# The first residual loads and three sums of leaves behind the first router, and the last block product added straight to the output

## The chip, the cores and the metric

The kernel runs on one core of a Trainium2 chip. The core has TensorE (matrix products, written PE in the profile, with its weight loads as PEld), VectorE (DVE), ScalarE (ACT), GpSimd (POOL) and SyncE (SP). SP, ACT and POOL also start DMA transfers, which move data between the memory of the chip and the core. All arithmetic here is in 32-bit floats.

The metric is the time of one execution on the device in microseconds, as the median of several runs. The profile comes from one further execution, and its times are counted from the start of its span.

## The reference

4096 tokens of width 1024 come in groups of 64; each group picks one of 16 matrices of 64 x 64, which mixes its 64 rows. On the mixed rows a router picks 16 of 64 experts per token, and two matrix products with gates between them are added to the input:

```python
W = weights[condition]                          # (64, 64, 64)
z = jnp.einsum('bct,bcd->bdt', x, W)            # mixed rows, 4096 x 1024
scores = z @ Wr.T                               # 64 experts
top_vals, top_idx = jax.lax.top_k(scores, 16)
gates = jax.nn.softmax(top_vals, axis=-1)       # scattered to G (4096 x 64)
h = jnp.einsum('nd,krd->nkr', z, A)             # 64 experts x rank 16 = 1024
out = jnp.einsum('nkr,kdr->nd', h * G[:, :, None], B)
return x + 2.0 * out
```

So the kernel computes two products of 1024 x 1024 for each token (by A, then by B) with the mixing, the router and the gates between them, and a sum with the residual x.

## The kernel before, in words

The tokens are worked on in 8 groups of 512. For each group there are two stages, `h` (x by A) and `o` (gated h by B). A stage is a product of 2 x 2 blocks, made from 7 block products p1 to p7 by the Strassen-Winograd scheme: sums of blocks go in, sums of products come out. The blocks of h are 256 tokens by 512 columns. From the second group on each of the 7 products is cut once more into 2 x 2 blocks and made from 7 "leaves" (so 49 small products for a stage); in the first group the products are whole (`whole_parent`, L529), while the sums of the leaves of A and B for all later groups are made and stored to memory beside them.

**The order of the work.** It is written out by hand. All products stand in one list `parents` (h0, o0, h1, h2, o1, h3, o2, and so on, o7 last), and `run` (L581) goes through them one after another. Each product has hooks: `mid`, `late` and `end` are lists of small jobs that `run` calls at three places of the product. `at(n, when, f, ...)` (L849) puts a job into a list. Each engine does its instructions in the order in which the program issues them, so a job's place in these lists is its place in the queue of its engine.

**In the first group,** with `h` and `o` the numbers of the first products of the two stages:

- `gather` (L153) starts the loads of the mixing matrices on POOL; `scores_t`, `turn`, `scores` (L172 to L230) make the router's scores.
- `route_top` (L232, at h+3) takes the 8 largest scores on VectorE, `exps` (L247) the exponentials on ScalarE, and `rest` (L257, at h+4) the next 8 with the sums and their reciprocals on VectorE. `scaled` (L285) multiplies the gates on ScalarE. `gates` (L297, at h+5) turns them with four transposes on TensorE (`gp`, L301), and `gated` (L308) mixes a quarter of z with 64 small products (`zp`, L321) and multiplies it by the gates on VectorE (`hb`, L334).
- `b_steps` (L890) is the list of the sums of leaves of B, 4 to each of the 7 products. Each is one subtraction on VectorE of 128 x 512 into a tile of the pool `bsum` (5 tiles), followed by a store to memory by POOL (`step`, L409, store at L414). `steps_of(lst, n)` takes the next n from the list. The table at L959 gives their places.
- `load_res` (L733) loads quarters of the residual x, 512 KB each, in the first group with POOL's queue, in later groups with SP's. They are added to on VectorE and stored as the output.

**A product of the second level** (`parent`, L474) has three accumulators x, y, w in the banks of TensorE. Its order in `run`: leaf p1 to x, ScalarE copies x to `r1`; p2 to y, VectorE makes the (0,0) quarter of the product as y + r1 (`part`, L603); then leaf p3 of the product before (`third`, L606), p6 on top of x and its copy `a`; leaf p4 of the product before (`fourth`, L610), whose quarter is w + a; p7 to w, p5 on top of x and its copy `b`, and the quarter (1,1) as w + b. The quarter (0,1) is x after p3. Then `done` of the product before adds it to its parts of the output, in `o_parents` (L776).

**The end.** The last product is p3 of the stage o of group 7. Its place in the output is the (0,1) quarter, an `o` tile of 2 x 128 tokens by 512. `finish` (L652) takes the quarters (0,0) and (1,1) from the product's tile, adds these and the copies a and b to the output, then makes leaf p3 in a bank of its own (`last_z`) and p4 on top of w, adds both, and stores the two halves with SP and ACT (L661). `late` (L786) adds product p5 to that quarter once p2, p5 and p4 are there.

Of the kernel before, what the change touches and what calls it, by code (L numbers as in the profile page):

```python
# [15 lines left out]
P = 128  # L16
BANK = 512
# [3 lines left out]
TPG = 4  # L21
CH = 4
HN = TPG * P // 2
HALF = BANK // 2
# [5 lines left out]
def kernel(  # L30
# [26 lines left out]
    nc = tc.nc  # L57
# [6 lines left out]
    NG = NT // TPG  # L64
# [21 lines left out]
    def add(o, a, b):  # L86
        nc.vector.tensor_tensor(o, a, b, ALU.add)  # L87
# [355 lines left out]
    parents, to_fetch, ring, stay, fetched = [], [], [], {}, [0]  # L443
# [137 lines left out]
    def run(par, before, after, hooks):  # L581


        two = par and par["level"] == 2
        tail = before and before["level"] == 2

        def bank(n):
            par["bank"][n] = acc.tile(
                [P, par["width"]],
                F32,  # L590
                tag="acc",
                name=f"{par['kind']}_{par['g']}_{par['j']}_{n}",
            )
            return par["bank"][n]

        def copied(n):
            lt = pools["lt"].tile(
                [P, HALF + KC], F32, tag=n, name=f"l_{n}", bufs=2 if n == "a" else 1
            )
            par["val"][n] = lt[:, : par["width"]]  # L600
            nc.scalar.copy(par["val"][n], par["bank"]["x"])  # L601

        def part(pr, i, j, n, v):  # L603
            add(pr["q"][i][j], pr["bank"][n], pr["val"][v])

        def third():  # L606
            before["mm"](before["bank"]["x"], "p3", False)
            nc.scalar.copy(before["q"][0][1], before["bank"]["x"])  # L608

        def fourth():  # L610
            before["mm"](before["bank"]["w"], "p4", False)
            part(before, 1, 0, "w", "a")

        if par:
            par["begin"]()
        if two:
            par["mm"](bank("x"), "p1", True)
            copied("r1")
            par["mm"](bank("y"), "p2", True)
            part(par, 0, 0, "y", "r1")  # L620
        elif par and hooks["both"]:
            par["both"]()
        elif par:
            par["half"](0)
        if before and not tail:
            before["done"](before["m"], before["v"])
        if tail:
            third()
        if two:
            par["mm"](par["bank"]["x"], "p6", False)  # L630
            copied("a")
        if tail:
            fourth()
        for f in hooks["mid"]:
            f()
        if after and after["level"] == 2:
            after["prepare"]()
        for f in hooks["late"]:
            f()
        if two:  # L640
            par["mm"](bank("w"), "p7", True)
            par["mm"](par["bank"]["x"], "p5", False)
            copied("b")
            part(par, 1, 1, "w", "b")
        elif par and not hooks["both"]:
            par["half"](1)
        if tail:
            before["done"](before["m"], before["v"])
        for f in hooks["end"]:
            f()  # L650

    def finish(par, st):  # L652

        o, q = st["os"][0, 1], par["q"]
        for s, k, v in ((0, 0, q[0][0]), (1, 1, q[1][1]), (0, 1, par["val"]["b"]), (1, 0, par["val"]["a"])):
            add(o[:, s, ts(k, HALF)], o[:, s, ts(k, HALF)], v)
        z = acc.tile([P, HALF], F32, tag="acc", name="last_z")
        for s, k, p, b, queue in ((0, 1, "p3", z, nc.sync), (1, 0, "p4", par["bank"]["w"], nc.scalar)):
            par["mm"](b, p, p == "p3")
            add(o[:, s, ts(k, HALF)], b, o[:, s, ts(k, HALF)])  # L660
            queue.dma_start(out[ts(st["g"] * TPG + s, P), ts(1, BANK)], o[:, s, :])  # L661

    def add_piled(o, piles, n):
        for s in range(2):
# [78 lines left out]
    def store(st, i, j):  # L743
        (nc.sync if st["g"] else nc.gpsimd).dma_start(
            out[ds((st["g"] * TPG + 2 * i) * P, 2 * P), ts(j, BANK)].rearrange(
                "(s p) t -> p s t", p=P
            ),
            st["os"][i, j],
        )
# [26 lines left out]
    def o_parents(st):  # L776

        m_ = {}

        def into(i, j, t, last=False):  # L780
            o = st["os"][i, j]
            add(o, o, t)
            if last:
                store(st, i, j)

        def late():  # L786
            if {"p2", "p5", "p4"} <= m_.keys():
                into(0, 1, m_["p5"])

        def done(j):  # L790
            def f(m, v):
                m_[j] = m
                if j == "p1":
                    into(0, 0, m)
                elif j == "p2":
                    into(0, 0, m, True)
                    late()
                elif j == "p6":
                    add(m_["p1"], m_["p1"], m)
                    into(1, 0, m_["p1"], {"p7", "p4"} <= m_.keys())  # L800
                elif j == "p4":
                    into(1, 0, m, {"p7", "p6"} <= m_.keys())
                    late()
                elif j == "p7":
                    into(1, 1, m)
                    into(1, 0, m, {"p4", "p6"} <= m_.keys())
                elif j == "p5":
                    assert {"p6", "p7"} <= m_.keys()
                    add(m, m, m_["p1"])
                    into(1, 1, m, True)  # L810
                    late()
                else:
                    into(0, 1, m, True)

            return f

        return [parent("o", st, j, lambda: st["h_ops"], done(j)) for j in ORDER["o"]]
# [14 lines left out]
    sts = [{"g": g} for g in range(NG)]  # L832
    for k, g in (
# [4 lines left out]
        st = sts[g]  # L838
# [10 lines left out]
    def at(n, when, f, *args):  # L849
        hooks[n][when].append(lambda: f(*args))  # L850
# [34 lines left out]
    def steps_of(lst, n):  # L885
# [4 lines left out]
    b_steps = [  # L890
        f for j in ("p1", "p2", "p3", "p7", "p5", "p6", "p4") for f in leaf_steps("o", j, br[j])
    ]
# [25 lines left out]
    st = sts[0]  # L918
    h, o = st["h"], st["o"]
# [38 lines left out]
    at(o + 3, "end", b_sums, 4)  # L958
    for k, lst, n in (  # L959
        (h + 2, b_steps, 4),  # L960
        (h + 3, b_steps, 5),
        (h + 4, b_steps, 3),
        (h + 5, a_steps, 4),
        (h + 6, a_steps, 5),
        (o, a_steps, 2),
        (o + 1, b_steps, 7),
        (o + 2, a_steps, 7),
        (o + 3, b_steps, 1),
        (o + 3, a_steps, 2),
        (o + 4, b_steps, 6),  # L970
        (o + 5, b_steps, 2),
    ):
        at(k, "end", steps_of, lst, n)
# [8 lines left out]
    h = sts[1]["h"]  # L982
# [5 lines left out]
    for st in sts[1:]:  # L988
        n, g = st["h"] + 7, st["g"]
# [33 lines left out]
    for st in sts:  # L1023
        g, h, o = st["g"], st["h"], st["o"]
        if not g:
            at(h + 2, "mid", load_res, st, (0, 0), (1, 1), (1, 0))
            at(o + 5, "mid", load_res, st, (0, 1))
        else:
            at(h - 1, "mid", x_operands, st)
            at(h + 1, "mid" if g < 3 else "late", sums, st, "x_sums", "s3")  # L1030
            at(h + 1, "end", sums, st, "x_sums", "s2")
            at(h + 2, "end", sums, st, "x_sums", "s1")
            at(h + 3, "end", sums, st, "x_sums", "s4")
            at(o - 2, "end", h_operands, st)
            at(o - 1, "end", sums, st, "h_sums", "s3")
            at(o + 0, "end", sums, st, "h_sums", "s2")
            at(o + 1, "end", sums, st, "h_sums", "s1")
            at(o + 3, "late", sums, st, "h_sums", "s4")
            for k, q in zip((-2, -1, 1, 2), QUARTERS):
                at(o + k if g + 1 == NG else o - 4, "mid", load_res, st, q)  # L1040
            if g + 1 < NG:
                at(h + 3, "mid", gather, g + 1)
                at(h + 3, "end", load_x, g + 1, 0, 0)
                at(h + 4, "end", load_x, g + 1, 1, 0)
                at(h + 5, "mid", load_x, g + 1, 1, 1)
                at(h + 6, "mid", load_x, g + 1, 0, 1)
    for n, par in enumerate(parents):
        if n == sts[1]["h"]:
            steady()
        after = parents[n + 1] if n + 1 < len(parents) else None  # L1050
        run(par, parents[n - 1] if n else None, after, hooks[n])
    finish(parents[-1], sts[-1])


_OUT = (64, 64, 1024)
# [41 lines left out]
```

## Time and profile before

| | us |
|---|---|
| median of 3 runs | 784.57 |
| the three runs | 784.48, 784.57, 785.79 |
| the profiled execution, its own time | 786.72 |
| its span, first to last instruction | 784.8 |
| TensorE busy | 772.8 |
| VectorE busy | 623.7 |
| ScalarE busy | 184.7 |
| DMA, mean rate | 266 GB/s |

Mean granted clock of TensorE over the span: 0.995 of full speed.

How to read it: part 1 of the page gives the busy time of each engine as a share of the span; part 2 cuts the span into 40 slices of 19.6 us and gives the busy share of each in tenths. Rows of the timeline give start, length, engine, line, operation, output <- inputs, shapes and count; a bracket holds the time that the engine stood idle before the row and what ended that. A line such as L87 or L90 belongs to a helper (`add`, `sub`), so rows are told apart by their tiles: `os_p_p` is a sum of leaves of B, `hs_p_p` one of A, `o_p_p` and `h_p_p` their places in memory, `lo_p_p` and `lh_p_p` the leaves loaded again, `l_r`, `l_a`, `l_b` the copies r1, a and b, `m_o_p` a product of the stage o, `o` a quarter of the output. Rows of the waits give the waiting engine and line, what ended the wait, the sum in us, how many and the longest. q1 is the DMA queue of SP, q0 that of POOL, q10 that of ACT.

### The profile page before, as it was taken

To read this page: it belongs to the slowest core of one execution; us is meant where nothing else is said; L and a number is where in the kernel's file an instruction comes from. 1 tells how busy PE (TensorE), PEld (TensorE's weight loads), DVE (VectorE), ACT (ScalarE), POOL (GpSimd) and SP (SyncE) were. 2 spreads that over 40 slices of the span, in tenths; PEclk is the share of its full clock that TensorE was granted. 3 is DMA by queue.
4 is the path that set the end of the run, shared out by engine and by line. 5 is a ranking of instruction groups with operands and counts; after the bars stand their busy time and mean duration, and the time that the engine had idled before them with its cause. 6 is when DMAs were issued, how large, how long until landed. Compare 5 with 4: busy or idle time off the path is not lost.

```text
span 784.8 us, 14669 instructions
## 1 busy us (share of the span) xinstructions
PE 772.8 (98%) x5348; PEld 612.4 (78%) x5348; DVE 623.7 (79%) x1310; ACT 184.7 (24%) x490; POOL 74.3 (9%) x103
## 2 busy tenths in 40 slices
PE   9989999999999999999999999999999999999996
PEld 5444448888888888887888888888888888888885
DVE  4788975678788868897788976888768887788986
ACT  1120002223122222322222222222222231222221
POOL 4334352000200020000200010000200000000000
PEclk9999999999999999999999999999999999999998
DMA  9968579656788858886788958799488893688995
GB/s 332 403 256 296 202 235 316 192 166 208 237 265 286 298 191 295 280 299 236 240 283 284 311 199 283 261 291 334 130 315 269 283 352 119 221 261 255 353 377 215
DMA packets 107607, 208.50 MB, mean 266 GB/s; under 512 B 11072, under 2 KB 27200, under 8 KB 106640
## 3 DMA queue, kind: packets, MB, share of 16 engines
q1 hardware_dynamic: 100496, 186.83, 70.7%
q0 software_dynamic: 6608, 19.95, 7.3%
q8 instruction: 43, 0.70, 0.4%
q10 hardware_dynamic: 432, 0.79, 0.3%
q14 instruction: 28, 0.23, 0.1%
HBM read 174.41 MB, written 33.11 MB: 264 GB/s over the span
## 4 chain that ended last, share of the span: by engine, by line
PE 90%; DVE 3%; issue 3%; POOL 2%; DMA 2%; ACT 0%; POOLq 0%; DVEq 0%
PE h_p_x L508 23%; PE o_p_x L508 20%; PE h_p_w L508 12%; PE o_p_w L508 10%; PE h_p_y L508 6%; PE o_p_y L508 5%; PE zp L321 4%; PE o_x L545 4%; PE o_w L545 2%; POOL w_st L157 1%; PE gp L301 1%; DMA cond_b<-in_cond_dram 1%; DVE o L87 1%; PE sw L221 1%; PE o_y L545 1%
## 5 line engine op out<-in xcount | busy, mean ns | idle before, releaser
L508 PE MATMUL o_p_x<-lo_p_p,l_t 128*128 128x256 f32 x584 | 142.8, 379 | 0.0
L508 PEld LDWEIGHTS o_p_x<-lo_p_p,l_t 128*128 128x128 f32 x584 | 111.0, 190 | 15.4
L87 DVE TENSOR_TENSOR o<-o,m_o_p 128x1024 f32<-128x1024 f32 (+1 forms) x67 | 78.8, 1194 | 0.9 <-DMA o<-in_x_dram 0.4
L157 POOL DMA_INDIRECT w_st<-in_cw_dram,idx x32 | 34.9, 1090 | 429.4 <-PE zp L321 413.4
L87 DVE TENSOR_TENSOR m_h_p<-h_p_w,l_a 128x272 f32<-128x272 f32 x49 | 21.5, 439 | 62.6 <-PE h_p_w L508 62.6
L87 DVE TENSOR_TENSOR m_h_p<-m_h_p,m_h_p 128x1088 f32<-128x1088 f32 x49 | 62.3, 1282 | 0.2
L508 PE MATMUL h_p_x<-a,l_t 128*128 128x272 f32 x224 | 60.5, 392 | 0.0
L508 PE MATMUL h_p_w<-lh_p_p,l_t 128*128 128x272 f32 x196 | 53.8, 397 | 0.0
L508 PE MATMUL h_p_x<-lh_p_p,l_t 128*128 128x272 f32 x196 | 52.9, 392 | 0.0
L508 PE MATMUL o_p_w<-lo_p_p,l_t 128*128 128x256 f32 x196 | 51.1, 383 | 0.0
L508 PEld LDWEIGHTS h_p_x<-a,l_t 128*128 128x128 f32 x224 | 42.6, 190 | 8.6
L334 DVE TENSOR_TENSOR hb<-zp,gg 128x512 f32<-128x512 f32 x64 | 39.9, 683 | 9.8 <-PE zp L321 9.8
L601 ACT COPY l_b<-h_p_x 128x272 f32<-128x272 f32 x49 | 18.9, 386 | 121.8 <-PE h_p_x L508 119.5
L508 PE MATMUL h_p_x<-at,l_t 128*128 128x272 f32 x168 | 45.4, 392 | 0.0
L508 PEld LDWEIGHTS h_p_x<-lh_p_p,l_t 128*128 128x128 f32 x196 | 37.2, 190 | 7.5
L601 ACT COPY l_b<-o_p_x 128x256 f32<-128x256 f32 x49 | 18.2, 372 | 103.8 <-PE o_p_x L508 103.8
L508 PEld LDWEIGHTS h_p_w<-lh_p_p,l_t 128*128 128x128 f32 x196 | 36.5, 191 | 7.0
L508 PEld LDWEIGHTS o_p_w<-lo_p_p,l_t 128*128 128x128 f32 x196 | 36.6, 190 | 5.2
L321 PEld LDWEIGHTS zp<-w_st,m_h_p 64*64 64x64 f32 x2048 | 32.5, 137 | 7.9 <-issue 7.7
L87 DVE TENSOR_TENSOR m_o_p<-o_p_w,l_a 128x256 f32<-128x256 f32 x48 | 20.3, 422 | 22.8 <-PE o_p_w L508 22.8
L508 PEld LDWEIGHTS h_p_x<-at,l_t 128*128 128x128 f32 x168 | 31.9, 190 | 6.6
L608 ACT COPY m_h_p<-h_p_x 128x272 f32<-128x272 f32 x49 | 18.9, 386 | 70.7 <-PE h_p_x L508 70.7
(172 smaller groups left out, 1387.9 us busy)
## 6 DMA issues: line engine op xcount, KB each, us to landing
lo_p_p<-o_p_p SPq DMA_DIRECT2D x280, 256.0 KB, 3.9
lh_p_p<-h_p_p SPq DMA_DIRECT2D x147, 272.0 KB, 5.3
lo_p_p<-in_b_t_dram SPq DMA_DIRECT2D x63, 256.0 KB, 4.0
x<-in_x_t_dram SPq DMA_DIRECT2D x31, 512.0 KB, 5.8
o<-in_x_dram SPq DMA_DIRECT2D x28, 512.0 KB, 7.3
out_dram<-o SPq DMA_DIRECT2D x27, 512.0 KB, 5.0
o_p_p<-os_p_p POOLq DMA_DIRECT2D x28, 256.0 KB, 4.0
b<-in_b_t_dram SPq DMA_DIRECT2D x4, 1024.0 KB, 19.6
```

The costliest lines, as they stand in the source:

```text
L87: nc.vector.tensor_tensor(o, a, b, ALU.add)
L157: nc.gpsimd.indirect_dma_start(out=w_st[:, i, :], out_offset=None, in_=cw, in_offset=bass.IndirectOffsetOnAxis(ap=idx[:, n : n + 1], axis=0),)
L221: nc.tensor.matmul(sw[r, i, ts(k, K // 2)].rearrange("p (d k) -> p d k", d=2), lhsT=ws[g][r, i, :], rhs=halves(st["z"][i // 2, k])[r, i % ...
L301: nc.tensor.transpose(gp[:, i, :], st["g2"][i].rearrange("p a k -> p (a k)"), ident)
L321: nc.tensor.matmul(zp[b][e * D : (e + 1) * D, c, s, :], lhsT=halves(z)[r, s, c // 2, ds(c % 2 * P + e * D, D)], rhs=ws[g][r, 2 * i + s, :] ...
L334: nc.vector.tensor_tensor(tokens(hb[j, i])[:, :, :, b, :], zp[b], g_ij[:, :, :, b, :], ALU.mult)
L508: nc.tensor.matmul(bank, lhsT=v[:, c, :], rhs=w[:, c, :width], start=first and c == 0, stop=c == 1, skip_group_check=True,)
L545: nc.tensor.matmul(piles[n, s], lhsT=left()[j][:, c, ts(s, P)], rhs=w, start=c == 0 and PILES[kind][j].isupper(), stop=c == CH - 1, skip_g ...
L601: nc.scalar.copy(par["val"][n], par["bank"]["x"])
L608: nc.scalar.copy(before["q"][0][1], before["bank"]["x"])
```

## The change

It has two places.

In the first group, the loads of three quarters of the residual move from the `mid` jobs of product h+2 to those of h+6, and three of the sums of leaves of B from the `end` jobs of h+3 to those of h+4. The number of loads, sums and stores stays as it was.

At the end, `run` treats the last product in another way. Its leaf p2 and its copy r1 are added to the output's (0,0) part by two adds, instead of being summed in the product's tile first. The step behind `after["prepare"]` goes to `finish` at once, after the product before has been added (`before["done"]`). `finish` adds the copy a, makes leaves p7 and p5 itself, adds w to the part (1,1), makes p3 and p4, and then adds b, the bank of p3, b again and w, with each half stored when its last add is done. `late` of the last group doesn't wait for p2 any longer, so p5 is added to the (0,1) quarter one product earlier.

```diff
@@ run
             par["mm"](bank("y"), "p2", True)
-            part(par, 0, 0, "y", "r1")
+            par["copied"] = copied
+            if after is None:
+                o = sts[-1]["os"][0, 1][:, 0, :HALF]
+                add(o, o, par["bank"]["y"])
+                add(o, o, par["val"]["r1"])
+            else:
+                part(par, 0, 0, "y", "r1")
...
+        if after is None:
+            before["done"](before["m"], before["v"])
+            bank("w")
+            return finish(par, before, sts[-1])
         if two:
             par["mm"](bank("w"), "p7", True)
@@ finish
-    def finish(par, st):
-
-        o, q = st["os"][0, 1], par["q"]
-        for s, k, v in ((0, 0, q[0][0]), (1, 1, q[1][1]), (0, 1, par["val"]["b"]), (1, 0, par["val"]["a"])):
+    def finish(par, before, st):
+
+        o, q, val = st["os"][0, 1], par["q"], par["val"]
+
+        def into(s, k, v):
             add(o[:, s, ts(k, HALF)], o[:, s, ts(k, HALF)], v)
+
+        def out_tile(s, queue):
+            queue.dma_start(out[ts(st["g"] * TPG + s, P), ts(1, BANK)], o[:, s, :])
+
+        into(1, 0, val["a"])
+        par["mm"](par["bank"]["w"], "p7", True)
+        par["mm"](par["bank"]["x"], "p5", False)
+        par["copied"]("b")
+        into(1, 1, par["bank"]["w"])
         z = acc.tile([P, HALF], F32, tag="acc", name="last_z")
-        for s, k, p, b, queue in ((0, 1, "p3", z, nc.sync), (1, 0, "p4", par["bank"]["w"], nc.scalar)):
-            par["mm"](b, p, p == "p3")
-            add(o[:, s, ts(k, HALF)], b, o[:, s, ts(k, HALF)])
-            queue.dma_start(out[ts(st["g"] * TPG + s, P), ts(1, BANK)], o[:, s, :])
+        par["mm"](z, "p3", True)
+        par["mm"](par["bank"]["w"], "p4", False)
+        into(0, 1, val["b"])
+        into(0, 1, z)
+        out_tile(0, nc.sync)
+        into(1, 1, val["b"])
+        into(1, 0, par["bank"]["w"])
+        out_tile(1, nc.scalar)
@@ o_parents, late
-            if {"p2", "p5", "p4"} <= m_.keys():
+            if {"p5", "p4"} | ({"p2"} if st["g"] + 1 < NG else set()) <= m_.keys() and "late" not in m_:
+                m_["late"] = True
                 into(0, 1, m_["p5"])
@@ the table of the sums of leaves
         (h + 2, b_steps, 4),
-        (h + 3, b_steps, 5),
-        (h + 4, b_steps, 3),
+        (h + 3, b_steps, 2),
+        (h + 4, b_steps, 6),
@@ the loads of the residual
-            at(h + 2, "mid", load_res, st, (0, 0), (1, 1), (1, 0))
+            at(h + 6, "mid", load_res, st, (0, 0), (1, 1), (1, 0))
             at(o + 5, "mid", load_res, st, (0, 1))
@@ the main loop
         run(par, parents[n - 1] if n else None, after, hooks[n])
-    finish(parents[-1], sts[-1])
```

## The prediction

> **What bounds the kernel now.** I began with the page's first two parts, to see which engine fills the span and where it doesn't.
>
> ```profile
> PE 772.8 (98%) x5348; PEld 612.4 (78%) x5348; DVE 623.7 (79%) x1310; ACT 184.7 (24%) x490; POOL 74.3 (9%) x103
> ...
> PE   9989999999999999999999999999999999999996
> ```
>
> TensorE is busy for 98% of the span, and its only thin slices are the third (39 to 59 us) and the last (765 to 785 us). The change removes no matmul, so it can gain only there. The waits of TensorE in the first 150 us come next; after that, no TensorE wait is longer than 0.4 us.
>
> ```profile
> PE gp L301 <- ACT g L289: 2.6, 1, 2.6
> ```
>
> The timeline of TensorE around this wait, with start, length, and in brackets the idle time before it and its releaser:
>
> ```profile
> 39.26 10.46 PE L545 MATMUL h_x<-at,x 128*128 128x512 f32 x24
> 52.28 1.21 PE L301 MATMUL gp<-ident,g 128*128 128x128 f32 x4 [2.56 <-ACT g L289]
> 53.42 1.99 PE L321 MATMUL zp<-w_st,m_h_p 64*64 64x64 f32 x64
> 55.34 4.39 PE L545 MATMUL h_x<-at,x 128*128 128x512 f32 x8
> 59.57 7.03 PE L545 MATMUL h_w<-a,sum_p 128*128 128x512 f32 x16
> ```
>
> TensorE stands still for 2.56 us until the gates of the first router arrive, and what follows is slow too: the 64 small products take 1.91 us from start to start, against 1.09 us for the same 64 at 69.96 us. The table by stretches has the granted clock in the column after POOL:
>
> ```profile
> 50.00:52.00 2.00, 0.00 (x0) 0.00 (x0) 1.74 (x12) 0.17 (x1) 0.00 (x0) 1.00 0.48 193
> 52.00:54.00 2.00, 1.72 (x24) 1.14 (x28) 2.00 (x2) 2.00 (x6) 0.00 (x0) 0.84 0.01 2
> 54.00:56.00 2.00, 2.00 (x56) 1.71 (x50) 1.97 (x4) 0.11 (x1) 0.94 (x2) 0.50 0.04 12
> ```
>
> The clock falls to half after the wait. Who makes the gates late is read from VectorE's timeline:
>
> ```profile
> 33.19 0.69 DVE L90 TENSOR_TENSOR os_p_p<-b 128x512 f32<-128x512 f32 x1 [1.11 <-DMA b<-in_b_t_dram]
> 33.91 1.42 DVE L90 TENSOR_TENSOR os_p_p<-b,os_p_p 128x512 f32<-128x512 f32 x2
> 40.36 0.69 DVE L90 TENSOR_TENSOR os_p_p<-b 128x512 f32<-128x512 f32 x1 [5.03 <-DMA o_p_p<-os_p_p]
> 40.97 0.60 DVE L243 MAX8 tops<-sc 128x8 f32<-128x64 f32 x4
> ...
> 45.86 0.69 DVE L90 TENSOR_TENSOR os_p_p<-b 128x512 f32<-128x512 f32 x1 [0.31 <-DMA o_p_p<-os_p_p]
> ```
>
> The scores had been ready since 32.8 us. The router waits in VectorE's queue behind a sum of leaves that stands 5.03 us for a buffer, whose store (GpSimd's queue, issued at 34.18 us) has to land. Two shares of the DMA time between 28 and 30 us show why that is slow (packets, MB, share of the 16 engines):
>
> ```profile
> q1 hardware_dynamic: 71, 0.53, 65.8%
> q0 software_dynamic: 72, 0.29, 37.1%
> ```
>
> The engines are full, and q0 is then carrying the three residual loads of 512 KB, issued at 22.67 us, the last of which takes 13.4 us to land; the leaf stores queue behind them. At the other end, VectorE's last rows:
>
> ```profile
> 776.37 3.14 DVE L87 TENSOR_TENSOR o<-o,m_o_p 128x1024 f32<-128x1024 f32 x4
> 779.43 0.42 DVE L87 TENSOR_TENSOR o<-o,l_b 128x256 f32<-128x256 f32 x1
> 779.77 0.42 DVE L87 TENSOR_TENSOR o<-o,l_a 128x256 f32<-128x256 f32 x1
> 780.10 0.42 DVE L87 TENSOR_TENSOR o<-last_z,o 128x256 f32<-128x256 f32 x1
> 780.44 0.41 DVE L87 TENSOR_TENSOR o<-o_p_w,o 128x256 f32<-128x256 f32 x1
> ```
>
> TensorE's last product ends at 777.64 us, but VectorE still adds until 780.85 us; the last store is issued at 780.88 us and lands 2.8 us later. VectorE sets the end.
>
> **Part 1, residual loads moved (`load_res` from h+2 to h+6).** Three loads leave GpSimd's queue ahead of all leaf stores and reappear behind twelve leaf stores and nine raw or h-leaf stores. Of the 1.5 MB, some 0.95 MB moved before 33.1 us (0.23, 0.29 and 0.25 in the stretches of 2 us from 26 to 32, the rest after); at about 0.40 MB per us, block b11 lands some 2.4 us sooner, at about 30.7 us, which is before VectorE is free (32.08 us). So the first three sums start at 32.1 us instead of 33.19: 1.1 us. The first leaf store is then issued at about 33.1 us with nothing ahead of it in q0. Its landing time isn't shown for that state. From below it is 2.8 us (the stores at 54.5 to 56 us, engines idle), from above 6.2 us (the store at 34.18 us with the loads still ahead of it). I take 4.5 us, the store issued at 41.35 us: SP's backlog beside it, no loads ahead. It lands at 37.6 us, so the fourth sum starts there and not at 40.36: 2.8 us earlier (4.5 to 1.1 for the two bounds).
>
> **Part 2, three sums moved behind the router.** 3 x 0.69 us and the 0.31 us wait at 45.86 leave the path before `rest`: from 43.5 to 46.47 us as it stood, 2.3 us. With part 1, `rest` starts 5.1 us earlier, at 41.4; the reciprocals end at 46.7 instead of 51.79 us. ScalarE first finishes a copy at 46.92 us (its row at 46.33, bound to TensorE), then makes the four gates by 48.2 us, and TensorE reaches the transposes at 49.6 us. The wait is gone with 1.4 us to spare. With the 6.2 us landing the first gate is there at 48.9: still no wait.
>
> The gain on TensorE, from 49.56 us (39.26 plus 24 matmuls at 0.429) to the row at 59.57: 10.0 us before. After: 4 transposes some 0.6 (weight loads of 0.138 each), 1.09 for zp, 3.63 for 8 matmuls behind a zp (71.05 to 74.68): 5.3 to 5.6. That is 4.4 to 4.7 us: 2.56 of wait, 0.5 of transposes paced by ScalarE, and about 1.5 of half clock (0.82 in zp, 0.60 in h_x).
>
> **A rule that weighs against the last term.** The row: half clock for 3.4 us, from about 53.4 to 56.8 (0.68 in the stretch of 1 us from 53, 0.50 in the two behind it, 0.62 in that from 56). The Trainium skill, "TensorE: Matmul & The Clock Gate", Part 1 (What's actually happening), says that the clock drops to 4/8 after an idle window of about 3.4 us and that this window runs free of the kernel's start. The length agrees with the row. But the gap here is only 2.56 us (3.7 with the sparse transposes), so by the rule another run, with the window lying otherwise, need not drop at all. By the row the drop is worth 1.5 us in each run; by the rule anything from 0 to 1.5 in the timed ones, and the three timed runs, 784.48, 784.57 and 785.79, are apart by about that much. No run here shows the clock of a timed run. I take 0.9 for the median.
>
> **Where the moved work goes.** VectorE has no idle time from 46.5 to 70.36 us, so I followed it on. The six sums now stand together before the adds to `m_h_p` and `hb` (49.0 to 53.3 us); with five buffers the sixth waits for the store of the first: 0 to 1.5 us. hb00 ends at 55.7 to 57.4 us; TensorE needs it at 66.43 - 4.6 = 61.8. VectorE is through with the h leaves at 67.9 (66.2 to 69.6); TensorE's second block product of the next stage (75.77 us) then needs the gated hb and its sum, 2.54 us of VectorE, by 71.1: VectorE has to be free by 68.4. It costs 0 to 1.2 us; I take 0.3. The residual loads, 3 x 0.75 us of GpSimd, now go out at about 64 to 66 us; behind them stand four h leaf stores and three raw leaves, which nobody needs before 77 us. The first residual is added at about 75 us; even with 9.5 us to landing it is there.
>
> **Part 3, the tail.** The add of p5 into the (0,1) quarter moves up into the pause at 772.7 to 773.9 us, where VectorE waited 0.77 us. The (0,0) quarter is no longer first made in `m`: one add of 0.42 and the later add become two, at 773.97 and 774.42. Then in VectorE's order: p4 of the product before 774.76; the 1024-wide add 775.2; `a` 776.34; bank w 776.68 to 777.10. TensorE's last product has to wait for this read (it overwrites the bank), so it starts at 777.16 instead of 776.51: 0.65 us lost, it ends at 778.29. Meanwhile `b` 777.02, z 777.46, `b` again 777.80; the last add waits for TensorE and runs 778.4 to 778.8. The last store is issued at 778.85, against 780.88: 2.0 us. Two small adds more than before (0.34 each) are inside. The stores are the same in number; the 512 KB one goes out 1.15 us earlier, and the 2.8 us to landing stay. Bounds: 1.4 us, if each dependent add costs another 0.1, to 2.3.
>
> **Sum.** Against the profiled execution (span 784.8, time 786.72): 3.1 + 1.5 - 0.3 + 2.0 = 6.3, so 780.4 us. The median of the timed runs is 2.15 us below the profiled one; with the half-clock term at 0.9 the gain is 5.7, and 784.57 - 5.7 = 778.9 us.
>
> **Rivals.**
> - Both parts work: 0.70. 778.9 us, own range 777.3 to 780.4.
> - The early gain is given back, since VectorE arrives late at the next stage or the wait for a buffer turns up again ahead of the router: only the tail is left, 784.57 - 2.0 to 2.8, about 782. For it: the landing of a store is the least known number, and VectorE's slack was 0.8 us at 71.16. Against it: the three sums alone, 2.3 us, nearly cover the 2.56. 0.12.
> - The tail gains nothing, since TensorE's new wait for the read of bank w and the chain of adds into one tile eat it: 784.57 - 3.7 = 780.9. Against it: 3.2 us lie between TensorE's end and VectorE's. 0.06.
> - No change that can be measured: both terms fail. 784.6. 0.05.
> - Slower: the first residual lands so late that VectorE, blocked in order at its add, delays hb10, which TensorE needs at 90.90 - 4.6 = 86.3 us. Each us after about 84.7 costs one us, and the gains of 5.7 are used up at 90.4 us, 27 us after the issue. The longest landing shown for these loads is 13.4 us. From 92 us on it would be past 786.2. 0.07.
>
> **How the numbers follow.** The predicted time is that of the first case. The range starts at 777.2 (all of the clock term, nothing late, and 0.3 of spread) and reaches to 782.3, which takes in the two half-gains; outside remain the last two cases and a rest of the others. 0.2% is 1.6 us, about what a measurement of this kernel can tell from no change. Faster: 0.70 + 0.11 + 0.06 = 0.87; the same: 0.06; slower: 0.07.
>
> **What would show it.** The wait of TensorE for g at L301 below 0.5 us and the clock at 1.00 from 50 to 60 us; the wait of 5.03 us for o_p_p near 2.5 to 3.5; MAX8 at about 38 us; the row h_w behind it at about 55 us; no new TensorE wait before 90 us. In the last 10 us, a wait of TensorE for VectorE of about 1.1 us before the last o_p_w, and 1.2 us from TensorE's end to the last store's issue. I'm wrong if the leaf store still takes over 6 us without the loads ahead of it, if TensorE stands at the second product of the o stage, or if a dependent add into the same tile costs clearly more than 0.42 us.

## The result, and the profile after

The changed kernel takes 780.6 us (median of 6 runs, 779.68 to 781.05) against 785.59 us for the kernel before on the same chip (6 runs, 784.48 to 786.71): a ratio of 0.9936, 95% interval 0.9923 to 0.9948, or 5.0 us less. The profiled execution took 780.21 us, with a span of 778.4 us against 784.8: 6.4 us less.

The first two parts of the page of the changed kernel, lines as in the prediction:

```profile
PE 770.6 (99%) x5348; PEld 610.9 (78%) x5348; DVE 623.8 (80%) x1310; ACT 184.5 (24%) x490; POOL 73.8 (9%) x103
...
PE   9999999999999999999999999999999999999997
```

The third slice is full. The waits of TensorE in the whole span, without one of 1.5 us at its very start that both kernels have, and below the dots the old one (total, number, longest):

```profile
PE o_p_w L508 <- DVE o L87: 0.9, 1, 0.9
PE h_w L545 <- DVE m_h_p L87: 0.7, 1, 0.7
...
PE gp L301 <- ACT g L289: 0.2, 1, 0.2
```

The wait for the gates is 0.2 us instead of 2.6. Two waits are new: one at the row `h_w` in the first group, and one before the last product. The timeline of TensorE shows the first of them in place:

```profile
39.31 10.46 PE L545 MATMUL h_x<-at,x 128*128 128x512 f32 x24
49.61 0.60 PE L301 MATMUL gp<-ident,g 128*128 128x128 f32 x4
50.14 1.16 PE L321 MATMUL zp<-w_st,m_h_p 64*64 64x64 f32 x64
51.23 3.70 PE L545 MATMUL h_x<-at,x 128*128 128x512 f32 x8
55.66 7.13 PE L545 MATMUL h_w<-a,sum_p 128*128 128x512 f32 x16 [0.73 <-DVE m_h_p L87]
```

The transposes follow the 24 products at once, and the 64 small products take 1.09 us from start to start, where they took 1.9. The granted clock, again in the column after POOL in the table by stretches, stays at full speed:

```profile
50.00:52.00 2.00, 2.00 (x68) 1.52 (x68) 2.00 (x4) 0.88 (x2) 0.40 (x1) 1.00 0.03 8
52.00:54.00 2.00, 2.00 (x6) 0.85 (x5) 1.89 (x3) 0.00 (x0) 1.69 (x4) 1.00 0.58 211
54.00:56.00 2.00, 1.27 (x4) 0.40 (x3) 1.68 (x3) 0.58 (x1) 1.30 (x4) 1.00 0.95 350
```

But the row `h_w` starts at 55.66 us, 3.9 us earlier than before (59.57), and not 4.6. What went otherwise is in VectorE's timeline:

```profile
31.99 0.69 DVE L90 TENSOR_TENSOR os_p_p<-b 128x512 f32<-128x512 f32 x1
32.72 1.42 DVE L90 TENSOR_TENSOR os_p_p<-b,os_p_p 128x512 f32<-128x512 f32 x2
39.73 0.69 DVE L90 TENSOR_TENSOR os_p_p<-b 128x512 f32<-128x512 f32 x1 [5.60 <-DMA o_p_p<-os_p_p]
40.34 0.60 DVE L243 MAX8 tops<-sc 128x8 f32<-128x64 f32 x4
...
54.32 0.69 DVE L90 TENSOR_TENSOR os_p_p<-b 128x512 f32<-128x512 f32 x1 [0.36 <-DMA o_p_p<-os_p_p]
54.93 1.28 DVE L87 TENSOR_TENSOR m_h_p<-m_h_p,h_w 128x512 f32<-128x512 f32 x2
```

The wait ahead of the router is still there. It has grown from 5.03 to 5.60 us, so MAX8 starts 0.6 us earlier than before, where I had 2.8. The router is ready in time only because three sums no longer stand between MAX8 and the reciprocals (experiment 2 puts them back). The six sums behind the router then push the adds to `m_h_p` to 54.93 us, and TensorE waits for the bank that these read.

The end of VectorE's and TensorE's work, with the issues of the last two stores:

```profile
771.65 1.23 DVE L87 TENSOR_TENSOR o<-o,m_o_p 128x1024 f32<-128x1024 f32 x1
...
773.46 0.42 DVE L87 TENSOR_TENSOR o<-o,l_b 128x256 f32<-128x256 f32 x1
773.60 1.13 PE L508 MATMUL o_p_w<-lo_p_p,sum_p 128*128 128x256 f32 x4 [0.93 <-DVE o L87]
...
774.77 0.42 DVE L87 TENSOR_TENSOR o<-o,o_p_w 128x256 f32<-128x256 f32 x1
775.22 0.35 ACTq L670 DMA_DIRECT2D out_dram<-o  x1
```

The 1024-wide add is out of the way early. TensorE waits 0.93 us, and one small add is left behind its last product.

**Where the 6.4 us come from.** TensorE is 3.91 us earlier at the row `h_w`, and still 3.80 us earlier at the first row of the second group (114.57 against 118.37). From the start of `last_z` to the issue of the last store it took 5.46 us before (775.42 to 780.88) and takes 3.57 now (771.65 to 775.22): 1.89 less. From that issue to the end of the span it was 3.92 us, now 3.18. The differences make 3.80 + 1.89 + 0.74 = 6.4. The last of them is no gain of the change: in the profiles of the experiments this time is 3.2 to 3.9 us.

### The profile page after: what moved, and what is told of

Same layout as the page of the kernel before. It is cut to its first block, busy times and chain, and to the rows that moved or that the text cites. A ratio compares the mean times of both kernels' runs of the same rounds, so it can differ in the third digit from the quotient of the medians.

```text
span 778.4 us, 14669 instructions
## 1 busy us (share of the span) xinstructions
PE 770.6 (99%) x5348; PEld 610.9 (78%) x5348; DVE 623.8 (80%) x1310; ACT 184.5 (24%) x490; POOL 73.8 (9%) x103
## 4 chain that ended last, share of the span: by engine, by line
PE 95%; DVE 3%; DMA 1%; issue 0%; ACT 0%; ACTq 0%; DVEq 0%
PE h_p_x L508 23%; PE o_p_x L508 20%; PE h_p_w L508 12%; PE o_p_w L508 10%; PE h_p_y L508 6%; PE o_p_y L508 5%; PE zp L321 4%; PE o_x L545 4%; PE h_x L545 3%; PE h_w L545 2%; PE o_w L545 2%; DMA x<-in_x_t_dram 1%; DVE o L87 1%; PE sw L221 1%; PE gp L301 1%; PE h_y L545 1%
## 5 line engine op out<-in xcount | busy, mean ns | idle before, releaser
L87 DVE TENSOR_TENSOR o<-o,m_o_p 128x1024 f32<-128x1024 f32 x65 | 78.0, 1219 | 0.6
```

## The experiments

Every time is compared with the kernel before in the same session. Its median moved between 784.7 and 786.2 us from session to session; the seventh experiment shows what may lie behind it.

**1. Only the loads back.** If the residual's loads hold up the leaf stores, putting them back must make the wait ahead of the router longer.

```diff
-            at(h + 6, "mid", load_res, st, (0, 0), (1, 1), (1, 0))
+            at(h + 2, "mid", load_res, st, (0, 0), (1, 1), (1, 0))
```

> The changed kernel with the three residual loads back at h+2; the sums of leaves and the end stay changed. My prediction (the loads hold up the first leaf store in q0) expects VectorE's fourth sum some 3 to 4 us later than it would be without the loads. The rival, from the profile of the changed kernel (the wait there is 5.60 us, no shorter): the loads don't matter for that wait; the fourth sum starts at about 40.4 us against 39.7, rest about 0.6 us later, and TensorE's wait for m_h_p grows from 0.7 to some 1.3 us. Then the span is 778.7 to 779.3 us and the time at most 1 us above that of the changed kernel.

Measured: 781.24 us (4 runs), ratio 0.9947 (0.9927 to 0.9966), which isn't told apart from the change's 0.9936. VectorE's timeline:

```profile
31.95 0.69 DVE L90 TENSOR_TENSOR os_p_p<-b 128x512 f32<-128x512 f32 x1
...
38.90 0.69 DVE L90 TENSOR_TENSOR os_p_p<-b 128x512 f32<-128x512 f32 x1 [4.80 <-DMA o_p_p<-os_p_p]
...
42.49 0.69 DVE L90 TENSOR_TENSOR os_p_p<-b,os_p_p 128x512 f32<-128x512 f32 x1 [0.45 <-DMA h_p_p<-hs_p_p]
```

With the loads ahead of it the first leaf store lands no later: the fourth sum starts at 38.90 us, even earlier than in the changed kernel. So taking the loads away shortened nothing, and my step for part 1 falls. This doesn't show that the loads hold up nothing where they are present: by the landings in the trace the store lands here at 38.88 us, 1.0 us behind the last of the three loads (37.87), and in the kernel before at 40.34, 1.9 us behind it (38.47), as in a queue that is worked off in order. It shows that without the loads something else holds the store as long. The first sums start at 31.95 us in this run too, so their earlier start isn't the loads' alone either.

**2. Only the sums back.**

```diff
-        (h + 3, b_steps, 2),
-        (h + 4, b_steps, 6),
+        (h + 3, b_steps, 5),
+        (h + 4, b_steps, 3),
```

> The changed kernel with the three sums of leaves back in front of rest (5 and 3); the loads and the end stay changed. If the sums are what took the router off the path, the reciprocals end some 2.4 us later, at about 50.9 us, TensorE waits about 1.7 us for the gates, and the wait for m_h_p is gone, since VectorE's work up to there is the same: the span is 1 to 1.7 us longer than 778.4, more (up to 3 us) where the clock drops as well. If the loads had done it, the span would stay near 778.4.

Measured: 781.9 us (10 runs, 780.97 to 784.22), ratio 0.9958 (0.9944 to 0.9972). TensorE's timeline:

```profile
50.91 1.21 PE L301 MATMUL gp<-ident,g 128*128 128x128 f32 x4 [1.07 <-ACT g L289]
...
56.67 3.60 PE L545 MATMUL h_w<-a,sum_p 128*128 128x512 f32 x8
```

Part of the wait for the gates comes back, 1.07 us, and the wait at `h_w` is gone. The row starts 1.0 us later than in the changed kernel. Three of its ten timed runs had a mean granted clock of 0.997 or less, and took 783.3 to 784.2 us; the others took 781.0 to 782.4. So it is the place of the sums that takes the wait away for good. No profile shows one of the three slower runs; a drop of the clock in them is read from their mean clocks and times alone.

**3 and 4. Each end of the kernel alone.** The first has the early part of the change and the end of the kernel before; the second has the end alone.

```diff
@@ 3: run and finish as before
-        if after is None:
-            before["done"](before["m"], before["v"])
-            bank("w")
-            return finish(par, before, sts[-1])
...
+    finish(parents[-1], sts[-1])
@@ 4: the table and the loads as before
-        (h + 3, b_steps, 2),
-        (h + 4, b_steps, 6),
+        (h + 3, b_steps, 5),
+        (h + 4, b_steps, 3),
...
-            at(h + 6, "mid", load_res, st, (0, 0), (1, 1), (1, 0))
+            at(h + 2, "mid", load_res, st, (0, 0), (1, 1), (1, 0))
```

> The kernel before with its own end, but with the loads and the three sums moved as in the changed one. The part of the end is then the difference to the changed kernel: I expect 2.0 us by my sum (span 780.4); by the two profiles, if the last stores land sooner too, up to 2.6 us (span 781.0). TensorE's h_w after the first gates starts at about 55.7 us.

> The kernel before with the changed end only. Span 784.8 less 2.0 to 2.6 us, 782.2 to 782.8; if the two parts are independent, its gain and that of the kernel with only the early part add up to that of the changed kernel. The wait of 2.6 us for the gates stays.

Measured: the early part alone 783.27 us (11 runs), ratio 0.9969 (0.9957 to 0.998); the end alone 782.66 us (8 runs), ratio 0.9967 (0.9955 to 0.9979). The gains, 0.0031 and 0.0033, add up to the 0.0064 of both together, so there is no sign that one part is given back in the other. Each interval is about 0.9 us to either side, so a loss of that size would not be seen. At 785.5 us the gains are 2.4 and 2.6 us.

The end alone has a surprise at its other side. TensorE waits for the gates there too, 1.84 us, but the clock stays at 1.00 in its profile from 50 to 58 us:

```profile
51.87 1.21 PE L301 MATMUL gp<-ident,g 128*128 128x128 f32 x4 [1.84 <-ACT g L289]
...
57.64 2.74 PE L545 MATMUL h_w<-a,sum_p 128*128 128x512 f32 x6
```

Only one of its eight timed runs had a mean clock as low as 0.996 (783.99 us). Its early instructions are those of the kernel before, where about half of the runs have one (experiment 7); whether that is chance, in eight runs, or has a cause is open.

**5. The router ahead of one more sum.** If the wait is for a store to land, the fourth sum should stand behind MAX8, so that nothing of the router waits for it. The fourth of the `h+2` jobs is moved to `h+3`:

```diff
-        (h + 2, b_steps, 4),
-        (h + 3, b_steps, 2),
+        (h + 2, b_steps, 3),
+        (h + 3, b_steps, 3),
```

> The changed kernel with one more sum moved: 3, 3 and 6 sums at h+2, h+3 and h+4, so that the sum that waits for its store's landing stands behind route_top. If VectorE's wait of 5.6 us is what makes its later adds to m_h_p late, the router's first part (2.3 us with the sum s4) now runs inside the wait: MAX8 at about 34.2 us, rest at about 41.8 instead of 43.5, the m_h_p adds at about 53.2, and TensorE's wait of 0.7 us for them is gone: h_w at about 54.95 and a span some 0.7 us under 778.4. If the bound is VectorE's work and not its wait, nothing is gained.

Measured: 779.09 us (4 runs, 779.06 to 779.25), ratio 0.9916 (0.9899 to 0.9933). VectorE and TensorE in the timeline:

```profile
33.96 0.60 DVE L243 MAX8 tops<-sc 128x8 f32<-128x64 f32 x4
...
39.32 1.33 DVE L90 TENSOR_TENSOR os_p_p<-b 128x512 f32<-128x512 f32 x2 [3.43 <-DMA o_p_p<-os_p_p]
...
54.67 7.03 PE L545 MATMUL h_w<-a,sum_p 128*128 128x512 f32 x16
```

The store lands as late as ever, but VectorE uses the time: it waits 3.43 us instead of 5.60. The adds to `m_h_p` start at 52.37 us, and the wait at `h_w` is gone.

**6. SP's leaf stores out of the way.** The other candidate for the late landing is SP's queue: behind the loads of B's blocks it carries six stores of 272 KB, the leaves of A. Four of them go to ScalarE's queue, behind the exponentials.

```diff
-    for d, t in to_store:
+    for d, t in to_store[4:]:
         nc.sync.dma_start(d, t)
...
     at(h + 3, "end", exps, st, 0, 1, 2, 3)
+    for d, t in to_store[:4]:
+        at(h + 3, "end", nc.scalar.dma_start, d, t)
```

> The changed kernel with four of the six stores of A's leaves (1.1 of 1.6 MB) taken from SP's queue and issued by ACT after the exponentials, at about 42.4 us. If these stores, which stand in SP's queue behind the blocks of B, are what the first leaf store in POOL's queue waits for, its landing falls from 6.7 to about 4 us or less, VectorE's wait from 5.6 to under 3.5 us, and TensorE's wait for m_h_p goes. If a store in POOL's queue takes over 6 us at any backlog there, the wait stays at 5 us or more.

Measured: 779.74 us (4 runs, 779.34 to 780.0), ratio 0.9925 (0.9908 to 0.9942). The shares of the DMA time from 34 to 36 us (packets, MB, share), first of the changed kernel, then of this one:

```profile
q1 hardware_dynamic: 377, 0.80, 105.8%
q0 software_dynamic: 1, 0.00, 0.5%
```

```profile
q0 software_dynamic: 142, 0.49, 63.0%
q1 hardware_dynamic: 60, 0.18, 22.4%
```

And VectorE's fourth sum in this kernel:

```profile
34.49 0.69 DVE L90 TENSOR_TENSOR os_p_p<-b 128x512 f32<-128x512 f32 x1 [0.16 <-DMA h_p_p<-hs_p_p]
```

In the changed kernel SP's queue takes the whole of the engines, and the first leaf store of B, issued at 32.98 us, moves all but nothing until 36 us and lands at 39.71, 6.73 us after its issue. With four of SP's stores out of the way it is issued at 33.18 and lands at 37.03: 3.85 us. So SP's backlog makes some 2.9 us of its landing in the changed kernel.

The wait falls further, from 5.60 to 0.16 us, for a second reason, which the bracket names: in this kernel the fourth sum waits for another store, one of A's leaves (`h_p_p<-hs_p_p`). That store is now the first in SP's queue, issued at 15.92 us instead of 25.28, and lands at 34.47. So the sum takes another buffer here, and 0.16 us does not measure the landing of B's leaf store. Waiting for that one it would have stood some 2.7 us (an estimate: from 34.33, when VectorE is free, to 37.03). MAX8 starts at 35.10, and `h_w` at 54.96 without a wait.

**7. The clock alone.** The kernel before, with TensorE kept busy in its gap: nine products of the identity with itself, which the transposes overwrite.

```diff
+        if not st["g"]:
+            for _ in range(9):
+                nc.tensor.matmul(gp[:, 0, :], lhsT=ident, rhs=ident, start=True, stop=True)
         for i in range(TPG):
```

> The kernel before with 9 products of the identity with itself (128 x 128, results overwritten by the transposes) ahead of the first gates' transposes. They fill some 2 us of TensorE's wait and take nothing off the path. If the two clusters of the times of before (about 784.3 and 786.5) are runs without and with the drop of the clock after this wait, only the lower one is left, a median of 784.0 to 784.6, and the granted clock stays at 1.00 from 50 to 60 us. If the clusters have another cause, both stay and the median stays at 785.5 to 786.

Measured: 784.72 us (22 runs) against 785.84 (27 runs), ratio 0.9987 (0.998 to 0.9994): 1.1 us. TensorE's timeline, in which the nine products are 18 instructions, and one stretch of the table:

```profile
49.68 2.17 PE L302 MATMUL gp<-ident 128*128 128x128 f32 x18
51.87 1.21 PE L304 MATMUL gp<-ident,g 128*128 128x128 f32 x4
...
57.64 2.74 PE L548 MATMUL h_w<-a,sum_p 128*128 128x512 f32 x6
```

```profile
54.00:56.00 2.00, 2.00 (x17) 0.97 (x10) 1.97 (x4) 0.00 (x0) 1.28 (x3) 1.00 0.25 94
```

The row `h_w` starts at 57.64 us instead of 59.57, 1.93 us earlier, with the clock at 1.00. Of this, 0.41 us is the gates, which happened to come earlier in this profile (the transposes start at 51.87 instead of 52.28), and 1.52 us is the clock. Experiment 4's profile has the same two starts, 51.87 and 57.64, with the gap left open and no drop. None of the filled kernel's runs had a mean clock below 0.997. Over the four sessions of the experiments the kernel before has 70 timed runs with their clock: 37 with a mean granted clock of 0.996 or less, median 786.5 us, and 33 with 0.997 or more, median 784.7. So the clock seems to drop in about half of the runs, and these are 1.8 us slower. That would also move the median of the kernel before: in the session with the lowest one, 784.7, only 3 of 8 runs are of the first kind, in the others more than half.

**8. A second improvement at the end, on top of 5.** GpSimd makes the one 1024-wide add into the last but one output quarter, so that VectorE is free sooner.

```diff
-            add(o, o, t)
+            if st["g"] + 1 == NG and (i, j) == (1, 1) and last:
+                nc.gpsimd.tensor_tensor(o, o, t, ALU.add)
+            else:
+                add(o, o, t)
```

> The kernel of e5_router_first with one add of the end moved from VectorE to GpSimd: p5 into the quarter (1,1) of the last group (128 x 1024). VectorE then starts the chain of the last adds 1.14 us sooner; the last stores go out 0.6 to 1.1 us earlier, if GpSimd's add doesn't slow VectorE and its store still lands before them. Time 778.8 to 779.5 us, against 780.6 for the changed kernel.

Measured: 780.46 us (6 runs), ratio 0.9936 (0.9921 to 0.995). From the start of `last_z` to the issue of the last store it takes 771.01 to 775.12, 4.11 us, against 3.58 in experiment 5. GpSimd's row and the row of VectorE beside it:

```profile
767.27 3.33 POOL L807 TENSOR_TENSOR o<-o,m_o_p 128x1024 f32<-128x1024 f32 x1 [204.64 <-DVE m_o_p L87]
769.01 1.87 DVE L87 TENSOR_TENSOR o<-o,l_r 128x256 f32<-128x256 f32 x1
```

A small add of two SBUF tiles, 0.42 us elsewhere, takes 1.87 us and ends at 770.88, just after GpSimd's add (770.60). The add before it, with one operand in a bank, keeps its 0.42. The Trainium skill, "SBUF — State Buffer", section "Who interferes with whom", says that a VectorE instruction with two SBUF inputs contends with a GpSimd instruction that reads SBUF, and that the ports that the two share are an exclusive lock. These rows agree. VectorE's own 1024-wide add at 767.16 us kept its usual 1.22, so a part of GpSimd's 3.33 us may be waiting too; that wasn't separated. The move gains nothing: the median is 1.4 us above experiment 5's in the same session.

**9. The loads on a third queue.** Is it the stores alone that SP's backlog holds, or any queue that joins late? The residual's loads are issued by ScalarE at the end of `h+2`.

```diff
-            (nc.sync if g else nc.gpsimd).dma_start(
+            (nc.sync if g else nc.gpsimd if (i, j) == (0, 1) else nc.scalar).dma_start(
...
-            at(h + 6, "mid", load_res, st, (0, 0), (1, 1), (1, 0))
+            at(h + 2, "end", load_res, st, (0, 0), (1, 1), (1, 0))
```

> The changed kernel with the three residual loads issued by ACT at the end of h+2 (the first at about 34 us, while the six stores of A's leaves drain from SP's queue). It asks what the stores of SP's queue hold up. If they hold up only other stores, the first load moves data from about 35 us on at a share of a third or more, while q0, with the first leaf store, still moves nothing until about 36 us. If whatever comes later has to wait for SP's backlog, q10 moves nothing until then either.

Measured, in one run: 781.12 us. The shares of the DMA time from 34 to 36 us, in which no line for ScalarE's queue, q10, appears, though its first load was issued at 34.01 us:

```profile
q1 hardware_dynamic: 356, 0.78, 102.9%
q0 software_dynamic: 8, 0.03, 4.0%
```

The loads don't move either: q10 has its first 13.7% between 36 and 38 us. Some of this is the usual start: in the changed kernel a store issued at 40.72 us, with the engines nearly idle, has its first packets at about 41.8 us, 1.1 us later. Here the first packet comes at 36.53, 2.5 us after the issue. The fourth sum waits 6.86 us. So in these kernels a queue that joins during SP's backlog is held, whether it loads or stores.

**10. Experiment 5 with the loads back.** Are the loads worth anything once the router is first?

```diff
-            at(h + 6, "mid", load_res, st, (0, 0), (1, 1), (1, 0))
+            at(h + 2, "mid", load_res, st, (0, 0), (1, 1), (1, 0))
```

> The kernel of e5_router_first with the residual loads back at h+2. If moving the loads is worth nothing, its time is that of e5_router_first, 778.8 to 779.6 us, with MAX8 at about 34 us. By my prediction, which gave the loads 1.1 us of start and 2.8 us of wait on VectorE's path, it would lose TensorE's gain of 0.7 us again and come out near 780 us.

Measured: 781.44 us (5 runs), ratio 0.9954 (0.9936 to 0.9971). Of the two outcomes named beforehand it is the second and more: slower than experiment 5. VectorE's timeline:

```profile
32.73 0.69 DVE L90 TENSOR_TENSOR os_p_p<-b 128x512 f32<-128x512 f32 x1 [0.58 <-DMA b<-in_b_t_dram]
...
43.08 0.69 DVE L90 TENSOR_TENSOR os_p_p<-b,os_p_p 128x512 f32<-128x512 f32 x1 [1.47 <-DMA h_p_p<-hs_p_p]
```

Block b11 is late again, and the last of the three sums waits 1.47 us for one of A's leaf stores. In this kernel q0, with the loads, has 34% to 41% of the engines from 28 to 34 us (nothing in experiment 5), and SP's stores end later: q1 still has 87% from 36 to 38 us, against 53%. The wait at `h_w` is back with 0.68 us, and the row starts at 55.78 us instead of 54.67. So moving the loads does pay once the router is first: 1.1 us by TensorE's row, and some 2 us by the medians, which come from other sessions. In the changed kernel itself, experiment 1 found no such difference.

**11 and 12. The change and experiment 5 once more, on one chip.**

> The changed kernel once more, beside e13 on the same chip: 779.7 to 781.1 us, as in its first six runs.

> The kernel of e5_router_first once more, beside the changed kernel on the same chip. By the profiles it should be 0.7 to 1.1 us faster than that; if the earlier difference (779.09 to 780.6, in different sessions) was the chip's, the two agree.

Measured: the change 781.21 us (6 runs, 780.82 to 781.43), ratio 0.9943 (0.9929 to 0.9957); experiment 5 779.62 us (6 runs, 779.39 to 780.84), ratio 0.9928 (0.9913 to 0.9943). The difference is 1.6 us, as it was across sessions (780.6 to 779.09: 1.5), though the intervals of the two ratios overlap. Side by side on one chip the runs hardly do: 780.82 to 781.43 against 779.39 to 780.84. Experiment 5 is the best version found.

## Why the prediction was right, and where it was not

The time was forecast at 778.9 us and is 780.6; the gain at 5.7 us and is 5.0. The other 1.0 us of the difference is the base: the kernel before took 784.57 us in three runs and 785.59 in six. The gain in span was forecast at 6.3 us and is 6.4. That the spans agree so well is partly luck: the early part gave 3.80 us instead of 4.3 (3.1 + 1.5 - 0.3), the end 1.89 instead of 2.0, and a last store that happened to land sooner made up for both with 0.74.

- **Part 1, the residual's loads: the step fell.** The failed term is the landing of the first leaf store without the loads ahead of it: I took 4.5 us (bounds 2.8 to 6.2), and it took 6.73. I had read the two shares at 28 to 30 us, where q0 held the residual, and took that to be all that stood in the way. I did not look at the same shares in the wait itself, from 36 to 38 us in the kernel before:

```profile
q1 hardware_dynamic: 368, 0.72, 93.6%
q0 software_dynamic: 33, 0.09, 11.4%
```

What I took off q0 was taken at once by SP's own queue, which rose from 66% to 99% at 28 to 30 us. Experiments 1 and 6 separate the two: with the loads back the store lands after 5.94 us, with four of SP's stores gone after 3.85. The first sums did start earlier, at 31.99 us instead of 33.19 (1.2, forecast 1.1), but with the loads back they start at 31.95 in experiment 1 and at 32.73 in experiment 10, so how much of this the loads give isn't settled.

- **Part 2, the three sums: right.** The sums alone were to cover nearly all of the 2.56 us, and they did: the reciprocals start 3.3 us earlier (48.12 instead of 51.41), and only 0.6 of it comes from MAX8. The wait at L301 is 0.2 us and the clock 1.00, both as forecast; MAX8 came at 40.34 us, not at about 38.
- **The missed step: the adds to `m_h_p`.** I wrote that the six sums "stand together before the adds to `m_h_p` and `hb`", and then followed only `hb`, with 4 us to spare, and the next stage. The adds to `m_h_p` read the bank that TensorE's `h_w` row writes next, so TensorE waits for them 0.73 us: a new wait before 90 us, which I had said would not be there. It is late because the router is late: with MAX8 at 33.96 or 35.10 us (experiments 5 and 6) it is gone.
- **The 0.3 us for VectorE's lateness at the second product of the o stage: 0.** VectorE is busy without a gap from 54.3 to 71.9 us, and TensorE's row there starts at 71.97 without a wait. It was closer than I knew: some 0.05 us are left.
- **The clock: right in kind, and in size within the interval.** The drop costs 1.5 us in the trace, as forecast. I took 0.9 of it for the median, between the row (a drop in each run) and the rule of the Trainium skill, "TensorE: Matmul & The Clock Gate", Part 1 (What's actually happening), by which the window runs free. From that I had inferred that a gap as short as this may or may not drop the clock. Experiment 7 gives 1.1 us (0.5 to 1.6), and the runs of the kernel before fall into two nearly equal parts, as a window that runs free could make them; the window itself no run here shows.
- **Part 3, the end: right.** 2.0 forecast; 1.89 us in the trace, with TensorE's wait at 0.93 (about 1.1). The end alone gains 2.6 us by its runs. That has a part of the clock's 1.8 in it, if it dropped in one of eight runs there and in half of those before: as an estimate 0.375 x 1.8 = 0.7, which leaves 1.9.
- **The median against the profile.** Of the 6.4 us in the spans, the profile of the kernel before has a whole clock drop, where the median has half, and 0.74 us in the landing of the last store. With half of 1.8 off for the first, 6.4 - 0.74 - 0.9 = 4.8, near the 5.0 of the medians (an estimate).
- **The early part as a whole** was forecast at 3.1 + 0.9 - 0.3 = 3.7 us of the median and gave 2.4 by experiment 3 (1.6 to 3.4 by its interval): the missed wait, 0.9 in that kernel's trace, may be most of the difference.
- **The rivals.** The wait for a buffer did turn up again ahead of the router, as the second case had it, but with the three sums moved it cost little; the residual's loads, issued at 65.04 us, were there when VectorE added to them at 75.94 us without a wait, so the slower case had no ground. (The longest landing of these loads in the kernel before was 14.3 us; the 13.4 that I gave is the median of the last two.)

## What to carry to other kernels

When an instruction waits for a buffer whose store is slow, look at the shares of all DMA queues in the very microseconds of the wait, not when the transfer ahead of it was running: taking work off one queue doesn't help if another queue has a backlog to fill the engines with. And read which store the waiting instruction needs: in experiment 6 a new order of the stores gave it another buffer. Here it was surer to move what must not wait ahead of the instruction that does than to try to shorten the wait: one sum moved behind the router gave 1.6 us, where moving 1.5 MB of loads had shown none in experiment 1. And when work is moved behind a critical step, list every reader of a bank that TensorE writes next, not only the producers of what it reads.

## What the runs showed that I had not expected

- One queue can all but stop while SP's queue drains a backlog of small packets. From 34 to 36 us SP's leaf stores moved 0.80 MB in 377 packets (about 2 KB each), q0 one packet and, in experiment 9, q10 none. It isn't only a queue that has just been given work: in the kernel before, q0 falls to 11.4% from 36 to 38 us with the last of the residual's loads still under way (it lands at 38.47). Nor is it always so: in experiment 1 q0 has 55.7% against 43.9% from 34 to 36 us. The Trainium skill, "DMA: Bandwidth & Descriptors", section "Queues, rings and completion order", says that each engine takes turns between its queues packet by packet; the last case looks like that, the other two don't. What makes the difference wasn't tried.
- A gap of TensorE well under 3 us can go with a lower clock: 2.56 us did in the profile of the kernel before, and by their mean clocks in 37 of its 70 runs. With gaps of 1.84 and 1.07 us in the profiles of experiments 4 and 2 it was one run of eight and three of ten. These are too few to say how the chance depends on the gap, and each gap is known from one profile.
- An add on GpSimd was not free for VectorE: one of 3.33 us stretched one of VectorE's from 0.42 to 1.87 us.
